# Linear attention block on one core: two sequences in turn, both chunks' scores and both chunks' weighted sums in one run each

## The chip, the core and the metric

The kernel runs on one NeuronCore of a Trainium2 chip (trn2), as one launch. The metric is the device time of that core in microseconds (us). Engines are named as in the profile: PE is TensorE (its weight loads are PEld), DVE is VectorE, ACT is ScalarE, POOL is GpSimd, SP is SyncE, which here issues the DMAs. All data are float32.

## The reference

The input x has 4 sequences of 2048 positions and 512 features. A layer norm comes first, then an attention with gates and no softmax, then a second layer norm and a feed-forward part of low rank, both with a residual. Cut to what matters (`gate` is divided by its mean over the features):

```python
xn = layernorm(layernorm(x)) * ln_g + ln_b           # outer and inner norm
q, k, v = split(xn @ W_qkv + b_qkv)
gate = sigmoid(layernorm(x) @ W_gate + b_gate)
q = relu(q * gate) ** 2 + EPS                        # 16 heads of 32
k = relu(k * gate) ** 2 + EPS
# along the sequence, for each head:
kv_s += k_t[:, None] * v_t[None, :];  k_s += k_t
out_t = (q_t @ kv_s) / (q_t @ k_s + EPS)
x = x + out @ W_proj + b_proj
x = x + gelu(layernorm(x) @ U1 @ V1 + b1) @ U2 @ V2 + b2
```

The recurrence couples positions within a sequence only; the four sequences are independent of each other.

## The kernel before

The 8192 rows are cut into 64 chunks of 128 positions, 16 to a sequence. The recurrence is computed by chunks. Within a chunk the scores (keys times queries, 16 small products of 32 rows by 128 columns, each two records on PE) are masked to the causal triangle on DVE (`scores_of`, L611) and multiplied with v; what came before the chunk enters as queries times the state S (`weighted`, L672); then S is brought up to date by k times v, accumulated in a PSUM bank of its own over a whole sequence and copied out after each chunk. The denominators come from a running sum of the keys (a scan on DVE, `sums_of`, L590) times the queries (POOL), summed over heads (`inverse_denominators`, L637).

The main loop (L1140) goes in steps of two chunks, c and c + 1, which before the change follow each other in one sequence. The large products of a pair of chunks are done by a scheme with seven half products in place of eight: `gates_and_values` and `queries_and_keys` (L435, L480; all at L426, seven groups each) and `project_two_out` (L762). A step does the following on PE, in this order: gates and values of c, c + 1; scores of e = c - 1; queries and keys of c, c + 1; `down` of the feed-forward part (ps_P, L844); rest of the attention of e (products with S, with v, state update); some feed-forward items; output projection of c - 2 and c - 1; scores of c; the other feed-forward items; rest of the attention of c; the two products `up` (ps_u, L883). So c + 1 has its scores and its rest a step later.

The feed-forward part works on blocks of two chunks (`feed_forward`, L837). It is a list of closures that `pump(n)` takes from, n at a time: `down`, then 16 products `hidden` (ps_h, L859), each followed by a gelu on ACT (L861), and 16 products `gather` (ps_Q, L865), each two behind its `hidden`; then two `up`, which also write the result out.

Queries, keys and normalized features are needed with features in partitions. They are turned over by a transpose of 32 by 32 blocks on DVE (L286), a write to DRAM (L302, L325) and reads back (L307: four reads of 32 partitions each; L330: one read of a chunk). `turned_in_quarters` issues the write and then every read that stands in the list `back` (`transfers_back`), and appends its own reads to that list. So a tile's reads are issued on SP behind the next write. `features_back` issues the reads of the next pair's features (xlT). The keys read back (kq) go through ACT (`keys_of`, L583: plus EPS, in order of time), then the scan and the scores.

The order of instructions on each engine is written out by hand (`manual_schedule`): each engine and SP's queue work in the order of the program, and semaphores make an instruction wait for what it reads and for buffers. PSUM before: 6 banks under one tag, one for the feed-forward sum (acc) and one for the state (S).

Of the kernel before, what the change touches and what calls it, by code (L numbers as in the profile page):

```python
# [60 lines left out]
def tile_linear_attention_block(  # L61
# [45 lines left out]
    def bank(name):  # L107
        return psum.tile([P, 512], F32, tag="bank", bufs=6, name=name)
# [3 lines left out]

    def load_x(c):
        t = xp.tile([P, D], F32, tag="x", name=f"x_{c}")
        nc.sync.dma_start(t, xf[bass.ts(c, P), :])
        x_of[c] = t
# [32 lines left out]
    bg_one = row(b_gate, "a", 4, "bg_one", nc.scalar)  # L149
# [25 lines left out]
    bqkv_one = [row(b_qkv[bass.ts(n, D)], "a", 4, f"bqkv_one_{n}", nc.sync) for n in range(3)]  # L175
# [236 lines left out]

    def combinations(c):
# [21 lines left out]
    def gates_and_values(c, s, meanwhile):  # L435
# [6 lines left out]
        nc.scalar.copy(t1, ps1)  # L442
        ps2 = bank(f"ps_gu_{c}")
        half_product(ps2, s[:, 1], wgv, T2)
        u2 = temp(f"gu2_{c}")
        nc.vector.tensor_add(u2, ps2, t1)
        ps5 = bank(f"ps_g_{c + 1}")
# [3 lines left out]
        meanwhile()  # L451
# [3 lines left out]
        done = [sigmoid_of(c, g0)]  # L455
        half_product(ps5, b[:, hi], wgv, T4, more=True)
# [11 lines left out]
        nc.vector.tensor_add(t5, ps3, bqkv_row[:, 2 * D : 3 * D])  # L468
        ps4 = bank(f"ps_v_{c}")
# [10 lines left out]
    def queries_and_keys(c, s, first=None, factors=None, queries=None, later=None):  # L480
# [9 lines left out]
        def square(c, n, t):  # L490
# [6 lines left out]
            sq = work.tile([P, D], F32, tag="k", bufs=3, name=f"k_{c}")  # L497
# [7 lines left out]
        if first:  # L505
            first()
# [5 lines left out]
        if factors:  # L512
            factors()
        nc.vector.tensor_add(t1, ps1, bq)
        q0 = square(c, 0, t1)
        if queries:
            queries()
# [5 lines left out]
        nc.gpsimd.tensor_add(u4, u2, t5)  # L523
        qT0 = turn_queries(c, q0)
# [4 lines left out]
        if later:  # L529
            later()  # L530
# [4 lines left out]
        nc.gpsimd.tensor_add(u3, u3, t5)  # L535
        half(ps5, b[:, NH:NK], T4, more=True)
        kq0 = turn_keys(c, k0)
        nc.vector.tensor_add(u2, ps5, u2)
        q1 = square(c + 1, 0, u2)
        k1 = square(c + 1, 1, u3)  # L540
        transfers_back()

        def second():
            qT1 = turn_queries(c + 1, q1)
            kq1 = turn_keys(c + 1, k1)
            pairs[c + 1] = k1, qT1, kq1
# [9 lines left out]
    def new_values(c):  # L556
        return work.tile([P, D], F32, tag="v", bufs=3, name=f"v_{c}")


    state = {"S": None, "sums": None, "bank": None}  # L560

    def turn_queries(c, q):
        qT = work.tile([P, NQ, NK, DH], F32, tag="qT", bufs=3, name=f"qT_{c}")
        turned_in_quarters(q, qT, f"q_{c}")
        return qT
# [7 lines left out]
    def new_keys(c):  # L573
        kT = work.tile([P, NK, P + 1], F32, tag="kT", bufs=2, name=f"kT_{c}")
        if c % SEQ == 0:
            nc.gpsimd.memset(kT[:, :, 0:1], 0.0)
        else:
            nc.gpsimd.tensor_copy(kT[:, :, 0:1], state["sums"][:, :, P : P + 1])  # L578
        return kT
# [10 lines left out]
    def sums_of(c, kT, qT):  # L590

        sums = work.tile([P, NK, P + 1], F32, tag="sums", name=f"sums_{c}")
        flat = "p g t -> p (g t)"
# [8 lines left out]
        state["sums"] = sums  # L602
        qs = work.tile([P, NK, P], F32, tag="qsum", name=f"qsum_{c}")
        nc.gpsimd.tensor_mul(  # L604
            qs.rearrange("p k (i t) -> p k i t", t=DH),
            qT.rearrange("p i k t -> p k i t"),
            sums[:, :, 1 : P + 1].rearrange("p k (i t) -> p k i t", t=DH),
# [3 lines left out]
    def scores_of(c, qT, kT):  # L611
# [3 lines left out]
        for g in range(NK):  # L615
            for r in range(HG):
# [7 lines left out]
                )  # L624
        scores = []
        for r in range(HG):
            a = work.tile([P, NK, P], F32, tag="a", bufs=4, name=f"a_{c}_{r}")
# [9 lines left out]
    def inverse_denominators(c, qs):  # L637

        back = work.tile([P, NK, P], F32, tag="back", name=f"back_{c}")
        nc.vector.transpose(back.rearrange("p g t -> p (g t)"), qs.rearrange("p g t -> p (g t)"))  # L640
        den = work.tile([P, H], F32, tag="den", bufs=2, name=f"den_{c}")
# [11 lines left out]
        den = inverse  # L653
        inv = work.tile([P, NK, P], F32, tag="back", name=f"inv_{c}")
        nc.vector.transpose(
            inv.rearrange("p g t -> p (g t)"), den.unsqueeze(2).to_broadcast([P, H, DH])
# [15 lines left out]
    def weighted(c, scores, qT, k, v, inv):  # L672


        S = state["S"]
        first = c % SEQ == 0

        num = [bank(f"ps_n_{c}"), bank(f"ps_m_{c}")]  # L680

        def place(g, r):
            at = r ^ (g % 2 * 2)
            return num[g % 2][at * DH : (at + 1) * DH, bass.ts(g // 2, P)]

        if not first:
            for g in range(NK):
                for r in range(HG):
                    rows = slice(r * DH, (r + 1) * DH)
                    nc.tensor.matmul(  # L690
                        place(g, r),
                        S[rows, g, :],
                        qT[rows, :, g, :],
                        start=(g < 2),
                        stop=False,
                        skip_group_check=True,
                    )
        for g in range(NK):
            for r in range(HG):
                h = g * HG + r  # L700
                nc.tensor.matmul(
                    place(g, r),
                    v[:, h * DH : (h + 1) * DH],
                    scores[r][:, g, :],
                    start=first and g < 2,
# [3 lines left out]
        if inv is None:  # L709
            return num  # L710
        oT = numerators_over(c, num, inv)


        if c % SEQ != SEQ - 1:
            if first:
                state["bank"] = psum.tile([P, 512], F32, tag="S", name=f"ps_S_{c}")
# [582 lines left out]
```

## Time and profile before

| what | value |
|---|---|
| time, median of 3 runs | 1780.97 us (1778.48 to 1781.12) |
| profiled execution, span from first to last instruction | 1778.1 us; no other time of it is given, so it is set beside the runs as 2.9 us under their median |
| PE busy | 1762.8 us, 99% |
| DVE, POOL, ACT busy | 1310.8, 832.4, 670.7 us |
| granted TensorE clock | 1.000 |
| DMA | 172.73 MB, mean 97 GB/s, 31.1% of 16 engines |
| a step of two chunks in steady state | 54.47 us |

The profile is one execution. Busy time counts an engine's instructions; the timelines list instructions of an engine in order of time, with start, length, source line, what is written from what, the shapes and how many records were merged. SP's lines are DMA issues, not transfers. The answer by windows gives, per stretch, its length, then the busy time and the instruction count of PE, PEld, DVE, ACT and POOL, then the granted clock, the DMA share of 16 engines and GB/s.

### The profile page before, as it was taken

What the parts mean: (1) busy time and instruction counts of PE and PEld (TensorE: products, weight loads), DVE (VectorE), ACT (ScalarE), POOL (GpSimd) and SP (SyncE); (2) the same over time, 40 slices, a digit from 0 to 9 for tenths busy, and PEclk for the clock granted to TensorE, in tenths of its full rate; (3) what the DMA queues carried; (4) which work ended last, traced back from release to release, by engine and by line L of the source; (5) the groups of instructions that cost most, each with busy time, mean ns of one, the idle gap of its engine ahead of it and who ended that gap; (6) DMA issues with size and microseconds to landing.
All of it is one profiled execution on the core that took longest, in us unless ns stands there. A gap on an engine that the chain in (4) does not pass through costs nothing.

```text
span 1778.1 us, 35487 instructions
## 1 busy us (share of the span) xinstructions
PE 1762.8 (99%) x13120; PEld 1135.1 (64%) x13120; DVE 1310.8 (74%) x2577; ACT 670.7 (38%) x1205; POOL 832.4 (47%) x1397
## 2 busy tenths in 40 slices
PE   9999999999999999999999999999999999999998
PEld 4555666656666666666566665666666666655677
DVE  7887777777777777777777777777777777777762
ACT  4333344333433333443334333333434343333333
POOL 3755455354553454543545534445435455344441
PEclk9999999999999999999999999999999999999999
DMA  7233332333323333323333233333233332332210
GB/s 231 80 101 92 104 101 91 98 95 100 108 87 97 103 91 105 101 91 98 92 103 103 91 98 104 90 107 101 88 99 93 104 102 90 97 103 79 85 61 24
DMA packets 284784, 172.73 MB, mean 97 GB/s; under 512 B 134590, under 2 KB 234430, under 8 KB 284484
## 3 DMA queue, kind: packets, MB, share of 16 engines
q1 hardware_dynamic: 283550, 170.46, 31.1%
q8 instruction: 104, 1.70, 0.4%
q14 instruction: 68, 0.56, 0.1%
q10 hardware_dynamic: 1062, 0.01, 0.0%
HBM read 89.15 MB, written 81.26 MB: 96 GB/s over the span
## 4 chain that ended last, share of the span: by engine, by line
PE 94%; DVE 3%; ACT 1%; DMA 1%; SPq 0%; issue 0%; POOL 0%; DVEq 0%; ACTq 0%; POOLq 0%
PE ps_h L859 13%; PE ps_Q L865 13%; PE ps_g L426 12%; PE ps_q L426 11%; PE ps_a L618 4%; PE ps_u L883 3%; PE ps_pt L426 3%; PE ps_pv L426 3%; PE ps_p L426 3%; PE ps_v L426 3%; PE ps_gt L426 3%; PE ps_u L426 3%; PE ps_gu L426 3%; PE ps_k L426 3%; PE ps_t L426 3%; PE ps_P L844 3%
## 5 line engine op out<-in xcount | busy, mean ns | idle before, releaser
L861 ACT ACTIVATE h<-ps_h,b_col 128x256 f32<-128x256 f32 x512 | 234.6, 470 | 331.1 <-PE ps_h L859 331.0
L859 PE MATMUL ps_h<-pT,v_sb 128*128 128x256 f32 x1024 | 300.5, 385 | 1.6 <-DVE pT L855 1.6
L865 PE MATMUL ps_Q<-h,u_sb 128*128 128x256 f32 x1024 | 298.6, 383 | 0.0
L604 POOL TENSOR_TENSOR qsum<-qT,sums 128x512 f32<-128x512 f32 x64 | 75.2, 1176 | 314.9 <-DVE sums L594 314.9
L865 PEld LDWEIGHTS ps_Q<-h,u_sb 128*128 128x128 f32 x1024 | 189.2, 190 | 40.4 <-ACT h L861 17.2
L859 PEld LDWEIGHTS ps_h<-pT,v_sb 128*128 128x128 f32 x1024 | 189.5, 190 | 32.1 <-DVE pT L855 3.0
L426 PE MATMUL ps_q<-wqk,xlT 128*128 128x512 f32 x372 | 177.9, 601 | 0.0
L628 DVE TENSOR_TENSOR a<-ps_a,causal 128x512 f32<-128x512 f32 x256 | 158.3, 680 | 23.5 <-PE ps_a L618 23.5
L426 PE MATMUL ps_g<-wgv,xlT 128*128 128x512 f32 x360 | 164.4, 592 | 0.0
L523 POOL TENSOR_TENSOR u<-u,t 128x512 f32<-128x512 f32 x32 | 40.6, 1268 | 208.6 <-DVE t L521 208.6
L570 POOL TENSOR_SCALAR k<-k 128x512 f32<-128x512 f32 x64 | 97.0, 1515 | 84.8 <-DVE blocks_k L286 84.8
L473 POOL TENSOR_TENSOR v<-gu,g 128x512 f32<-128x512 f32 x30 | 38.1, 1271 | 192.7 <-DVE g L468 192.7
L426 PEld LDWEIGHTS ps_g<-wgv,xlT 128*128 128x128 f32 x360 | 68.3, 190 | 85.7 <-issue 85.6
L426 PEld LDWEIGHTS ps_q<-wqk,xlT 128*128 128x128 f32 x372 | 68.1, 189 | 78.4 <-issue 53.1
L405 ACT ACTIVATE gate<-gate 128x512 f32<-128x512 f32 x64 | 40.3, 630 | 192.3 <-DVE gate L401 192.3
L494 ACT ACTIVATE t<-t,rg 128x512 f32<-128x512 f32 x32 | 23.1, 722 | 215.7 <-DVE t L492 215.7
L286 DVE STREAM_TRANSPOSE blocks_x<-x 128x512 f32<-128x512 f32 x60 | 42.0, 701 | 73.5 <-ACT x L267 73.5
L226 DVE BATCH_NORM_STATS2 st<-x 128x6 f32<-128x512 f32 x128 | 86.5, 676 | 8.6 <-DMA x<-in_L_attn_x_dram 6.4
L498 ACT ACTIVATE k<-u,rg 128x512 f32<-128x512 f32 x64 | 45.7, 714 | 120.7 <-DVE u L492 120.7
L594 DVE TENSOR_TENSOR_SCAN sums<-keep,kT 128x516 f32<-128x516 f32 x64 | 78.8, 1231 | 15.1 <-POOL kT L578 14.2
L618 PEld LDWEIGHTS ps_a<-qT,kT 32*128 32x128 f32 x2048 | 63.8, 186 | 35.9 <-issue 27.4
L982 POOL TENSOR_TENSOR x<-x,bp_row 128x512 f32<-128x512 f32 x64 | 81.4, 1272 | 0.0
(196 smaller groups left out, 3635.7 us busy)
## 6 DMA issues: line engine op xcount, KB each, us to landing
x<-in_L_attn_x_dram SPq DMA_DIRECT2D x64, 256.0 KB
dr_q<-blocks_q SPq DMA_DIRECT2D x64, 256.0 KB
dr_k<-blocks_k SPq DMA_DIRECT2D x64, 256.0 KB
qT<-dr_q SPq DMA_DIRECT2D x256, 64.0 KB
kq<-dr_k SPq DMA_DIRECT2D x256, 64.0 KB
out_dram<-x SPq DMA_DIRECT2D x64, 256.0 KB
dr_x<-blocks_x SPq DMA_DIRECT2D x60, 256.0 KB
x2T<-dr_x SPq DMA_DIRECT2D x240, 64.0 KB
```

The source lines that it names most:

```text
L226: nc.vector.bn_stats(st, src)
L426: nc.tensor.matmul(ps, stationary[:, k, :], w[:, slot, k, :], start=(k == 0 and not more), stop=(k == NH - 1), skip_group_check=True,)
L570: nc.gpsimd.tensor_scalar_add(k, k, EPS)
L594: nc.vector.tensor_tensor_scan(sums.rearrange(flat), keep.rearrange(flat), kT.rearrange(flat), 0.0, ALU.mult, ALU.add,)
L604: nc.gpsimd.tensor_mul(qs.rearrange("p k (i t) -> p k i t", t=DH), qT.rearrange("p i k t -> p k i t"), sums[:, :, 1 : P + 1].rearrange("p ...
L618: nc.tensor.matmul(ps[r][:, bass.ts(g, P)], kT[rows, g, 1 : P + 1], qT[rows, :, g, :], start=True, stop=True,)
L628: nc.vector.tensor_tensor(a, ps[r].rearrange("p (g t) -> p g t", t=P), causal.unsqueeze(1).to_broadcast([P, NK, P]), ALU.mult,)
L844: nc.tensor.matmul(ps, u1_sb[:, k, :], x2T[:, :, :, k, :].rearrange("p j i t -> p (j i) t"), start=(k == 0), stop=(k == NK - 1),)
L859: nc.tensor.matmul(ps, v1_sb[:, 0, bass.ts(f, P)], held["p"], start=True, stop=True)
L861: nc.scalar.activation(h, ps, AF.Gelu_apprx_tanh, bias=b1_col[:, f : f + 1])
L865: nc.tensor.matmul(held["q"], u2_sb[:, f, :], held["h"].pop(f), start=(f == 0), stop=(f == NF - 1))
L982: nc.gpsimd.tensor_add(x_of[e], x_of[e], bp_row)
```

## The change

Chunks are numbered anew: two sequences run in turn, so that c and c + 1 are at the same time in two sequences (`rows_of_chunk`, used by the loads and stores of x). The state S and the carried sums of keys exist twice. In each step, now d = c - 2:

- the scores of c and c + 1 stand together near the end of the step, masked by eight operations on DVE into eight tiles (`a`, before four);
- the rest of the attention of d and d + 1 stands together in the gates of the next step: products with S for both, then for each chunk four products with v and four state updates in turn; the update goes to a bank taken for this step and is added to S in SBUF on DVE, in place of accumulating in PSUM;
- the output projection has another order, with three `hidden` behind its first half product; `down` stands within the queries and keys;
- the normalized features of the feed-forward part are turned in the gates, those of the next pair within the queries and keys;
- in `second`, keys go ahead of queries; keys and sums of c + 1 move into the step that made them;
- PSUM has 8 banks under one tag; ACT copies ps_Q.

```diff
+    def time_of(c):
+        return c % RUN // NS
+    def rows_of_chunk(c):
+        return bass.ts((c // RUN * NS + c % NS) * SEQ + time_of(c), P)
...
         def second():
+            kq1 = turn_keys(c + 1, k1)
             qT1 = turn_queries(c + 1, q1)
-            kq1 = turn_keys(c + 1, k1)
             pairs[c + 1] = k1, qT1, kq1
...
+        if time_of(c) != SEQ - 1:
+            carries[c] = work.tile([P, NK, 1], F32, tag="carry", bufs=2, name=f"carry_{c}")
+            nc.gpsimd.tensor_copy(carries[c], sums[:, :, P : P + 1])
+        qs = sums[:, :, 1 : P + 1]
...
+        for s in range(NS):
             for g in range(NK):
                 for r in range(HG):
+                    h = g * HG + r
                     nc.tensor.matmul(
+                        place(s, g, r),
+                        v[s][:, h * DH : (h + 1) * DH],
+                        scores[s][r][:, g, :],
...
+                if not last:
+                    add_to_state(s, g)
+            inv = spread_inverse(c + s, inverse[s])
+            out.append(numerators_over(c + s, num[s], inv))
+        if not last:
...
+                nc.vector.tensor_add(S, product, S)
...
+    def scores_in_step(c):
+        ps = [scores_of(n, pairs[n][1], keys.pop(n)) for n in (c, c + 1)]
+        scores[c] = [masked(c + n, p) for n, p in enumerate(ps)]
...
     for c in range(NJ, NC, 2):
-        e = c - 1
+        d = c - 2
+        def features_and_attention():
+            second_features()
+            rest_of_attention(d)
...
+            hooks = {4: features_and_attention}
+        gates_and_values(c, combos[c], hooks)
...
         rest += feed_forward((c - 4) // NP)
+        second = queries_and_keys(
+            c,
+            combos.pop(c),
+            {
+                1: lambda: run(normalize_pair(c + 2)),
+                5: lambda: pump(1),
+                6: lambda: combine_results(d),
+            },
+        )
+        features_back()
         second()
+        for n in (c, c + 1):
+            keys[n] = new_keys(n)
+        project_two_in_step(d, lambda: pump(3))
+        transfers_back()
         for n in (c + 4, c + 5):
             first_moments(n)
...
         if c + 2 < NC:
             combine(c + 2)
+        pump(5)
+        sums_and_products(c)
+        pump(4)
+        denominators_in_step(c)
+        pump(10)
+        sums_and_products(c + 1)
+        waiting += second_norm([d, d + 1], mv_second, others, mv_first)
+        for n in (c, c + 1):
+            offset_in_residual(n)
+        pump(len(rest) - NP)
+        scores_in_step(c)
+        denominators_in_step(c + 1)
+        if c + 2 == NC:
+            second_features()
+        pump(len(rest))
```

A hook's number tells after which half product of the seven it runs. `sums_and_products(n)` issues `keys_of` on ACT, the scan on DVE and the product with the queries on POOL.

## The prediction

> **What bounds the kernel now.** I read the page's busy times first, then TensorE's timeline over one step, then SyncE's (SP's) timeline over the same step, then the DMA share by microsecond.
>
> ```profile
> PE 1762.8 (99%) x13120; PEld 1135.1 (64%) x13120; DVE 1310.8 (74%) x2577; ACT 670.7 (38%) x1205; POOL 832.4 (47%) x1397
> ```
>
> PE has 15 us of idle time in 1778.1. So two things can move the time: work leaves PE, or a wait appears in front of it. The table of waits puts no wait of PE in the steady steps over 0.4 us.
>
> TensorE's timeline (start, length, line, what, records) around the second chunk's attention and one run of scores:
>
> ```profile
> 770.96 1.89 PE L844 MATMUL ps_P<-x2T,u_sb 128*128 128x256 f32 x8
> ...
> 773.13 0.29 PE L690 MATMUL ps_n<-qT,S 32*32 32x128 f32 x4
> ...
> 773.38 0.42 PE L701 MATMUL ps_n<-a,v 128*32 128x128 f32 x8
> 773.62 0.40 PE L701 MATMUL ps_m<-a,v 128*32 128x128 f32 x8
> ...
> 774.27 0.49 PE L720 MATMUL ps_S<-v,k 128*32 128x32 f32 x32
> 774.73 1.56 PE L859 MATMUL ps_h<-pT,v_sb 128*128 128x256 f32 x6
> ...
> 786.74 0.59 PE L865 MATMUL ps_Q<-h,u_sb 128*128 128x256 f32 x2
> 787.26 1.17 PE L618 MATMUL ps_a<-qT,kT 32*128 32x128 f32 x32
> 788.36 0.70 PE L859 MATMUL ps_h<-pT,v_sb 128*128 128x256 f32 x2
> 788.90 0.59 PE L865 MATMUL ps_Q<-h,u_sb 128*128 128x256 f32 x2
> ```
>
> To be seen: two L865 records take 0.43 us, so the scores were due at 787.17 and start at 787.26; after them the first full-array product takes 0.54 (788.36 to 788.90) in place of 0.43. Every change of the array's tiling costs time at its edges.
>
> SP's timeline, same step. I call T0 the end of the products of queries and keys, 770.96:
>
> ```profile
> 772.46 0.33 SPq L302 DMA_DIRECT2D dr_k<-blocks_k  x1
> 772.95 2.25 SPq L307 DMA_DIRECT2D qT<-dr_q  x4
> 775.32 2.17 SPq L307 DMA_DIRECT2D kq<-dr_k  x4
> 777.61 2.32 SPq L330 DMA_DIRECT2D xlT<-drn_xl  x2
> 780.03 0.67 SPq L302 DMA_DIRECT2D dr_q<-blocks_q  x1
> 780.79 0.38 SPq L302 DMA_DIRECT2D dr_k<-blocks_k  x1
> 787.96 2.19 SPq L307 DMA_DIRECT2D qT<-dr_q  x4
> 790.26 2.26 SPq L307 DMA_DIRECT2D kq<-dr_k  x4
> ```
>
> To be seen: the write of the second chunk's queries, issued at 780.03, has landed only at 787.96, when SP may issue the reads. SP's table of waits has this each step ("DMA dr_q<-blocks_q: 212.4, 33, 8.0"). The DMA share by microsecond, where 0.25 is 4 of 16 engines:
>
> ```profile
> 785.00:786.00 1.00, 1.00 (x6) 0.89 (x5) 0.86 (x2) 0.73 (x2) 0.00 (x0) 1.00 0.27 84
> ...
> 792.00:793.00 1.00, 1.00 (x6) 0.87 (x5) 0.90 (x5) 0.61 (x2) 0.72 (x4) 1.00 0.25 76
> ...
> 795.00:796.00 1.00, 1.00 (x6) 0.79 (x5) 0.00 (x0) 0.80 (x2) 1.00 (x2) 1.00 0.22 65
> 796.00:797.00 1.00, 1.00 (x38) 0.47 (x40) 0.59 (x1) 1.00 (x3) 0.92 (x2) 1.00 0.02 6
> ```
>
> The eight quarter-reads run from 789 to 796 at a share of 0.25: about 3.5 us for four, and whatever waits behind them on those engines waits its turn. In the last step, which reads no xlT, the same reads are issued at 1708.12, 11.7 us after its ps_P at 1696.4; here it is 17.0. So the two xlT reads delay what follows them by 5.3 us. Today nobody needs these chunks before the next step.
>
> **The change, part by part.**
>
> *Scores of both chunks together.* A run costs, from when it is due (787.17) to when the second product after it has its usual place (788.90 - 0.43 = 788.47), 1.30 us. Its steady part I take from the products with v, which also stream 128 columns on four tiles: 8 records in 0.22 (773.62, 773.84 and on), so 32 in 0.88. Two runs in one save 1.30 - 0.88 = 0.42 us per step, on PE.
>
> *The rest of both together.* One run now lasts from 772.69 (770.96 + 8 x 0.216) to 774.73, plus 0.11 for the slow first product: 2.15. Steady parts: products with S 8 records in 0.11, so 0.44; with v 0.88; state updates 0.30 from first start to last (0.49 less 0.196, one record's length). Sum 1.62; the second run in the same block saves 0.53 us.
>
> *State updates among products with v.* Same number of records, and both are 128*32 tiles; the border from L701 to L720 shows no gap (774.06 + 0.22 = 774.28, start 774.27). The border back, L720 to L701, hardly stands in the trace. Bounds: a gain of 0.3 per chunk if the updates hide wholly, a loss of 0.11 per border (one load of L720) x 4 x 2 = 0.9 per step. I take 0, by the border that is shown. The Trainium skill (TensorE: Matmul & The Clock Gate, section on packing small matmuls) says that a weight load overlaps running matmuls only where the row group differs; these tiles use all four row groups, so by it every load would show, 0.11 x 32 = 3.5 us per chunk for the products with v alone. The trace has 0.88 for them, so the row decides.
>
> *PE's other work is the same* in kind and number. The wait of 0.25 after the first three ps_h (774.73 to 776.27 for 1.30 of work) loses most of its cause, as output products now follow them: 0.15. Gain on PE together 0.42 + 0.53 + 0.15 = 1.1 us; a step of 54.47 (ps_u starts at 689.41 and 743.88) would be 53.4 without new waits.
>
> *DVE* loses a copy (two of 0.28 become one add, 0.42 by the row of half-bank adds); *POOL* gains a carry copy per chunk (0.19), *ACT* the copy of ps_Q (0.37). All beside PE: cover is DVE's idle quarter and ACT's 62%. Without cover they'd cost about 1 us per step.
>
> *The feature transfers of x2T* move to the fourth hook of the gates; ps_P follows 17 us later on PE. The normalization waits for the gate's sigmoid, 2 us into that; write and eight reads take some 11 (2 x 0.7 transposes, 2 to land, 7 of reads). Slack about 4 us: nothing.
>
> *Keys and scores of c+1 move into their own step.* This is the new wait. Before, L583 for c+1 stood at the step's end (796.99) and its scores in the next step (812.21). After, PE has from T0: one half product 0.86, three ps_h 1.30, six half products 5.19, then 5 + 4 + 10 feed-forward items of 0.432 = 8.2: at T0 + 15.6 the keys of c+1 are queued on ACT. ACT works in order: the gelu of ps_h 12 and all later ones stand behind. PE has five more items (h12, g10, h13, g11, h14: 2.16) and at T0 + 17.7 it needs that gelu.
> When do the keys come? SP's order is kept: dr_k (T0 + 1.5), reads of qT and kq, two xlT reads, then the second chunk's writes at T0 + 9.1. The keys now go first, so their reads take the place of those at 787.96: T0 + 17.0. Four reads last till about 792.6 (half of 789 to 796): T0 + 21.7. Then L583 0.71, gelu 0.47, some 0.3 for hand-overs: T0 + 23.2. PE stands still 5.5 us. Behind it wait the last gathers, both scores and ps_u; the scan on DVE also waits, with nothing but masks behind it. The second qT lands by the same rows at T0 + 25.2 (796.1); the scores of c+1, then due at about T0 + 26.5, just escape. Even with keys on time, that qT alone would hold them from T0 + 20.9 to 25.2, 4.3 us: two waits with one cause.
> Bounds of the stall: 4.0 (reads a microsecond earlier, no hand-overs) to 6.5 (write landing at 8.0, the longest wait).
> As to the rule: the Trainium skill (DMA: Bandwidth & Descriptors, Bandwidth) gives 2.0 us plus bytes at 436 GB/s for a DMA, 2.6 for 256 KB. By it the keys' write would land at about T0 + 12 and the keys at T0 + 15, before ACT asks, and the change would be worth its 1.1 us per step, some 1748 in all. The row at 787.96 stands against it.
>
> *Clock.* The granted clock is 1.00 all through. At the start, the first eight ps_g took 5.98 us where eight later ones took 3.70 (chain of waits, 9.37 and 16.46): a cold array costs 2.28. An idle gap of 2.61 us (before ps_P at 118.12) cost nothing: its eight records took 1.97. A gap of 5.5 lies beyond what is shown; bounds 0 and 2.28 per step, I take half, 1.15. The Trainium skill (TensorE: Matmul & The Clock Gate, Part 1) puts the idle window at about 3.4 us; by it such a gap slows PE in many steps, not in all.
>
> **Sum.** A step is 53.4 + 5.5 = 58.9 (+4.4), with the clock +5.55. Steps c = 4 to 60 read xlT: 29. 29 x 5.55 = 161; the last step gains 1.1; prologue and tail have the same work in another order, 0 with bounds of 10 either way. 1778.1 + 160 = 1938; the runs' median lies 2.9 above the span: 1941, rounded to 1940. Without clock loss 1907, with all of it 1974.
>
> **The rivals.**
> *No wait (faster):* the second chunk's keys land before T0 + 16.5 and its queries before T0 + 20.9. Then 30 x 1.1 = 33 us are won: 1748. For it speaks the last step's 11.7 us; against it, that this step alone has no xlT reads ahead, while SP's order in the others stays. It decides at about 5 us less. Chance 0.08.
> *A shorter wait* of 1.2 to 4 us, if the landing of the first write runs ahead of the second xlT read: 1785 to 1860. 0.10; a wait of 1.1, which cancels the gain, 0.02.
> *More than one wait:* a slow clock in every step and exposed loads at the borders (0.9): 29 x (4.4 + 2.28 + 0.9) = 220, so 2000 and up. 0.08.
> *Forecast:* 0.72, its own range 1865 to 1985.
>
> The range takes the forecast and the upper part of the shorter wait: 1860 to 1990. Faster 0.08, same 0.02, slower 0.90, where 0.2% (3.6 us) is about what a measurement of this kernel can tell from no change.
>
> **What would show it.** Right: PE idle some 5 us before L865-type records in each step, released by ACT's gelu, with ACT idle before the keys' activation, released by a DMA of kq; PE busy near 92%; score runs of 64 records in 2.2 us or less. Wrong: PE at 98 to 99% and steps of 53.4 (no wait), or gaps inside the v and update records, or before ps_P (x2T late), or a wait that sits at the scores alone.

## Result and the profile after

The changed kernel takes 2014.59 us, median of four runs (2010.96 to 2023.08), against 1779.72 (1778.39 to 1781.12) for the kernel before on the same chip: ratio 1.1329, 95% interval 1.1302 to 1.1357. Slower was forecast, 1940 us and at most 1990. The profiled execution spans 2009.1 us, against 1778.1.

The page's busy times, then, in the table of waits (us in total, times, longest), PE's two largest and ACT's for the keys:

```profile
PE 1813.1 (90%) x13120; PEld 1173.4 (58%) x13120; DVE 1319.6 (66%) x2515; ACT 673.6 (34%) x1237; POOL 880.8 (44%) x1457
```

```profile
PE ps_Q L891 <- ACT h L887: 158.0, 44, 6.1
PE ps_S L723 <- issue: 7.5, 7, 1.8
```

```profile
ACT kT L597 <- DMA kq<-dr_k: 219.3, 63, 7.0
```

PE executes as many records as before and is idle for 196 us in place of 15. It is also busy for 50 us more. So there are two losses: a wait, in which `gather` (L891, L865 before) stands for a gelu, and PE working at a slower pace. The mean granted clock is 0.950, where it was 1.000. A third, small line is new: 7.5 us in front of the state updates, which the profile ascribes to no releaser ("issue").

One step shows the wait; T0, the end of the products of queries and keys, is at 815.2. SP's timeline:

```profile
816.92 0.33 SPq L311 DMA_DIRECT2D dr_k<-blocks_k  x1
...
822.34 1.58 SPq L339 DMA_DIRECT2D xlT<-drn_xl  x2
824.02 0.61 SPq L311 DMA_DIRECT2D dr_k<-blocks_k  x1
824.73 0.38 SPq L311 DMA_DIRECT2D dr_q<-blocks_q  x1
832.00 2.19 SPq L316 DMA_DIRECT2D kq<-dr_k  x4
834.30 2.29 SPq L316 DMA_DIRECT2D qT<-dr_q  x4
```

The second chunk's keys are written behind the two reads of xlT, and the write has landed only 8.0 us later, when the reads start at T0 + 16.8. ACT's timeline, then PE's:

```profile
837.70 0.72 ACT L597 ACTIVATE kT<-kq,eps_col 128x512 f32<-128x512 f32 x1 [6.02 <-DMA kq<-dr_k]
838.33 1.19 ACT L887 ACTIVATE h<-ps_h,b_col 128x256 f32<-128x256 f32 x3
```

```profile
832.67 0.59 PE L891 MATMUL ps_Q<-h,u_sb 128*128 128x256 f32 x2
833.11 0.59 PE L885 MATMUL ps_h<-pT,v_sb 128*128 128x256 f32 x2
838.83 1.22 PE L891 MATMUL ps_Q<-h,u_sb 128*128 128x256 f32 x2 [5.13 <-ACT h L887]
839.85 1.06 PE L885 MATMUL ps_h<-pT,v_sb 128*128 128x256 f32 x2
840.70 2.53 PE L891 MATMUL ps_Q<-h,u_sb 128*128 128x256 f32 x6
843.16 2.07 PE L635 MATMUL ps_a<-qT,kT 32*128 32x128 f32 x64
```

The keys' activation is at T0 + 22.5, three gelus queue behind it, and PE stands still for 5.13 us. Then ten full-array records take 4.33 us, from 838.83 to 843.16, where ten at full speed take 2.16 (about 0.43 for two, as between the starts at 832.67 and 833.11). The answer by windows gives the reason in the seventh group after the window, the clock (then DMA share and GB/s):

```profile
833.00:834.00 1.00, 0.70 (x4) 0.27 (x2) 0.00 (x0) 0.00 (x0) 1.00 (x2) 1.00 0.17 52
838.00:839.00 1.00, 0.17 (x1) 0.17 (x2) 0.59 (x2) 1.00 (x3) 0.00 (x0) 0.50 0.29 86
841.00:842.00 1.00, 1.00 (x4) 0.73 (x4) 0.00 (x0) 0.47 (x1) 0.95 (x1) 0.50 0.02 8
845.00:846.00 1.00, 1.00 (x11) 0.52 (x7) 1.00 (x3) 0.00 (x0) 0.71 (x4) 1.00 0.00 0
```

PE comes out of the gap at half its clock. It does so in every one of the 29 steps that read xlT: the records of the clock give half speed once in each, for 3.4 or 6.8 us (here from 836.0, still within the gap, to 842.8), 188 us in these steps.

What the change was said to save on PE is saved. Both chunks' scores take 2.1 us, as the line at 843.16 shows, and the rest of both chunks is one block. PE's timeline in the step before, its first and last parts:

```profile
793.78 0.43 PE L737 MATMUL ps_n<-a,v 128*32 128x128 f32 x8
794.02 0.24 PE L723 MATMUL ps_S<-v,k 128*32 128x32 f32 x8
794.08 0.41 PE L737 MATMUL ps_m<-a,v 128*32 128x128 f32 x8
...
795.99 0.24 PE L723 MATMUL ps_S<-v,k 128*32 128x32 f32 x8
796.16 1.12 PE L438 MATMUL ps_g<-wgv,xlT 128*128 128x512 f32 x2
```

Eight groups of products and updates take 2.38 us, 793.78 to 796.16; by the prediction's rows it was 2 x (0.88 + 0.30) = 2.36 with borders at nothing.

**The account.** Counted from one first record of ps_P to the next, a step has a mean length of 61.85 us over the 29 that read xlT, against 54.42 before (54.47 is the usual one, some are shorter): 29 x 7.43 = 215 us. Outside those steps the span is 1778.1 - 29 x 54.42 = 199.9 before and 2009.1 - 29 x 61.85 = 215.5 after: 16 us, of which 8.0 lie ahead of the first ps_P (118.1 before, 126.1 after). Together 231, the difference of the spans.

### The profile page after: what moved, and what is told of

Its sections match the earlier page's. It is cut to its first block, busy times and chain, and to the rows that moved or that the text cites. A ratio compares the mean times of both kernels' runs of the same rounds, so it can differ in the third digit from the quotient of the medians.

```text
span 2009.1 us, 35689 instructions
## 1 busy us (share of the span) xinstructions
PE 1813.1 (90%) x13120; PEld 1173.4 (58%) x13120; DVE 1319.6 (66%) x2515; ACT 673.6 (34%) x1237; POOL 880.8 (44%) x1457
## 4 chain that ended last, share of the span: by engine, by line
PE 69%; DMA 17%; DVE 5%; issue 3%; SPq 2%; POOL 1%; ACT 1%; ACTq 0%; DVEq 0%; POOLq 0%
DMA dr_k<-blocks_k 12%; PE ps_q L438 10%; PE ps_g L438 10%; PE ps_Q L891 6%; DMA kq<-dr_k 5%; PE ps_h L885 4%; PE ps_a L635 3%; PE ps_u L906 3%; PE ps_p L438 3%; PE ps_P L870 3%; PE ps_t L438 3%; PE ps_k L438 3%; PE ps_u L438 3%; PE ps_gu L438 2%; PE ps_v L438 2%
## 5 line engine op out<-in xcount | busy, mean ns | idle before, releaser
L891 PE MATMUL ps_Q<-h,u_sb 128*128 128x256 f32 x1024 | 347.9, 438 | 158.7 <-ACT h L887 158.0
L891 PEld LDWEIGHTS ps_Q<-h,u_sb 128*128 128x128 f32 x1024 | 219.1, 220 | 216.4 <-ACT h L887 182.5
L887 ACT ACTIVATE h<-ps_h,b_col 128x256 f32<-128x256 f32 x512 | 222.3, 471 | 216.6 <-PE ps_h L885 216.4
L885 PEld LDWEIGHTS ps_h<-pT,v_sb 128*128 128x128 f32 x1024 | 202.8, 198 | 32.1 <-DVE pT L881 1.9
L660 DVE STREAM_TRANSPOSE back<-sums 128x512 f32<-128x512 f32 x64 | 45.1, 705 | 222.4 <-POOL sums L621 222.4
L430 POOL TENSOR_TENSOR combos<-xlT 128x256 f32<-128x256 f32 x31 | 22.5, 726 | 320.5 <-DMA xlT<-drn_xl 242.0
L850 POOL TENSOR_TENSOR x<-x,b_row 128x512 f32<-128x512 f32 x64 | 80.4, 1279 | 185.4 <-ACT x L276 185.4
L597 ACT ACTIVATE kT<-kq,eps_col 128x512 f32<-128x512 f32 x64 | 46.2, 722 | 219.3 <-DMA kq<-dr_k 219.3
L584 POOL TENSOR_SCALAR k<-k 128x512 f32<-128x512 f32 x64 | 107.9, 1699 | 6.1 <-DVE blocks_k L295 3.6
L621 POOL TENSOR_TENSOR sums<-qT,sums 128x512 f32<-128x512 f32 x64 | 74.9, 1171 | 45.8 <-DMA qT<-dr_q 35.5
```

What stands on the lines that cost most here:

```text
L584: nc.gpsimd.tensor_scalar_add(k, k, EPS)
L621: nc.gpsimd.tensor_mul(qs.rearrange(by_quarter, t=DH), qT.rearrange("p i k t -> p k i t"), qs.rearrange(by_quarter, t=DH),)
L850: nc.gpsimd.tensor_add(xt, xt, b2_row)
L885: nc.tensor.matmul(ps, v1_sb[:, 0, bass.ts(f, P)], held["p"], start=True, stop=True)
L887: nc.scalar.activation(h, ps, AF.Gelu_apprx_tanh, bias=b1_col[:, f : f + 1])
L891: nc.tensor.matmul(held["q"], u2_sb[:, f, :], held["h"].pop(f), start=(f == 0), stop=(f == NF - 1))
```

## Experiments

The first four runs ask what makes PE stand and what it costs, a fifth (queries first) turns one part of the change back, and the others try the version without the wait and its parts. Ratios are to the kernel before on the same chip, whose median was between 1779.3 and 1780.5 us each time.

**Features last.** The reads of xlT go behind the second chunk's transfers, and the sums for the gates, which read xlT, are formed later.

```diff
-        features_back()
         second()
...
         transfers_back()
+        features_back()
...
-        if c + 2 < NC:
-            combine(c + 2)
...
         sums_and_products(c + 1)
+        if c + 2 < NC:
+            combine(c + 2)
```

> The reads of the next pair's features (xlT) are issued behind the reads of the second chunk's keys and queries, and the sums on POOL that need them stand behind the keys' sums. Theory A (the new wait comes from the keys of c + 1, which queue behind the two xlT reads on a quarter of the DMA engines): their write lands at about T0 + 11, the first read is issued there, L597 for c + 1 starts at about T0 + 16 instead of 22.5, the gap before ps_Q falls from 5.2 us to under 0.7, the granted clock stays at 1.00; a step is 53.5 to 54.3 us, the run 1765 to 1795 us. Theory B (the gap comes from ACT's order or from PSUM banks of the merged scores, whatever the DMAs do): gap and time as they are, 2000 to 2020 us.

Measured: 1840.69 us, ratio 1.0347 (1.0327 to 1.0368), clock 0.996, a step 55.93. SP's timeline in a step with T0 at 747.7, and the new wait of PE's weight loads:

```profile
755.19 0.60 SPq L311 DMA_DIRECT2D dr_k<-blocks_k  x1
755.89 0.38 SPq L311 DMA_DIRECT2D dr_q<-blocks_q  x1
759.52 2.19 SPq L316 DMA_DIRECT2D kq<-dr_k  x4
```

```profile
PEld ps_gu L438 <- POOL combos L431: 46.4, 29, 2.2
```

The second chunk's keys are read from T0 + 11.8 and not from T0 + 17; the gap ahead of `gather` falls from 5.2 us to 0.2 in the mean, and no step is at half clock any more. Moving the two reads in SP's queue, with the sums that need them, brings 174 of the 235 us. The run misses its expected time by 46 us, above all by a wait that the move makes: xlT now lands about T0 + 25, and the gates of the next step stand for the sums formed from it, 0.77 us of PE per step. With 0.56 that is left ahead of `gather`, most of it at the first chunk's keys, and 0.36 in gaps without a releaser, that is 1.7 of the 2.5 us by which the step exceeds the 53.43 reached below; the rest is in no gap above 50 ns and stays open.

**Features spread.** xlT is still read first, but each chunk as four reads of 32 partitions. The source then has 32 rows as its slowest dimension, where it had 4.

```diff
+            for j in range(NQ):
                 nc.sync.dma_start(
-                    new_tile().rearrange("p k t -> p (k t)"),
-                    dr.rearrange("m j k i t -> j m (k i t)"),
+                    to[j * DH : (j + 1) * DH, :],
+                    dr[:, j].rearrange("m k i t -> m (k i t)"),
                 )
```

> The place of the xlT reads is kept, but each is issued as four reads of 32 partitions, whose slowest dimension is 32 and no longer 4. Theory A1 (a read whose slowest dimension is 4 runs on 4 engines, and the second chunk's writes wait behind it on those): DMA share in the xlT reads well over 0.5, SP spends about 2 us more on issues, the second chunk's write still lands 3 to 4 us earlier, gap about 1.6 us, clock near 1.00, 1810 to 1850 us. Theory A2 (the xlT reads delay by their bytes or by the order of the queue, on however many engines): the landing stays at T0 + 17 or later, 2000 to 2060 us.

Measured: 1894.6 us, ratio 1.0647 (1.0629 to 1.0664). First the share of the 16 DMA engines (windows, last figures but one) while the xlT reads are under way, in the changed kernel and in this run, then SP's timeline in this run (T0 at 769.2):

```profile
828.00:830.00 2.00, 2.00 (x11) 1.77 (x10) 0.52 (x1) 1.02 (x3) 0.00 (x0) 1.00 0.26 99
```

```profile
777.20:779.20 2.00, 2.00 (x11) 1.77 (x10) 1.83 (x5) 0.95 (x2) 0.00 (x0) 1.00 0.69 178
```

```profile
776.33 4.15 SPq L341 DMA_DIRECT2D xlT<-drn_xl  x8
780.58 0.37 SPq L311 DMA_DIRECT2D dr_k<-blocks_k  x1
781.04 0.38 SPq L311 DMA_DIRECT2D dr_q<-blocks_q  x1
782.72 2.19 SPq L316 DMA_DIRECT2D kq<-dr_k  x4
```

The write behind the reads lands after 2.1 us in place of 8.0. Part of that is a later issue: eight issues of 0.52 us keep SP until 780.5, so the write is issued 2.6 us later in the step than in the changed kernel (T0 + 11.4 against 8.8). Counted from the first issue of the xlT reads, the keys' reads start after 6.4 us in place of 9.7, with the same bytes ahead of them: what held the write was the reads' tail on some 4 of 16 engines, not their bytes.

A gap of about 2 us stays, where 1.6 was expected, and the clock is not near 1.00 throughout: 14 of the 29 steps have half clock, 13 of them after gaps of 1.92 to 2.61 us. The run misses its range by these two. Two gaps of the same length in PE's timeline, and a window behind each (the clock is the third figure from the end):

```profile
848.28 0.70 PE L894 MATMUL ps_Q<-h,u_sb 128*128 128x256 f32 x2 [2.61 <-ACT h L890]
```

```profile
1601.22 0.70 PE L894 MATMUL ps_Q<-h,u_sb 128*128 128x256 f32 x2 [2.61 <-ACT h L890]
```

```profile
849.00:851.00 2.00, 2.00 (x17) 1.40 (x20) 0.14 (x1) 0.70 (x2) 0.83 (x2) 1.00 0.08 24
1602.00:1604.00 2.00, 2.00 (x6) 1.65 (x5) 0.07 (x1) 0.47 (x1) 0.93 (x2) 0.50 0.09 26
```

Of the 22 steps whose longest gap lies between 1.92 and 2.64 us, 13 have half clock and nine do not; of the six with 1.40 to 1.85 us none has.

The Trainium skill (DMA: Bandwidth & Descriptors, "Why a DMA increments its semaphore by 16 and not by 1") says that a copy runs on the largest number of engines, up to 16, that divides the slowest dimensions of both sides; 4 and 32 rows would then give 4 and 16 engines, which the share of 0.26 there and 0.69 here, more than 4 of 16 could give, agree with. The reads of keys and queries also have 4 in that place in the code (each takes 32 rows of the DRAM tile and writes all 128 partitions), and ran at 0.25 in the prediction's windows; no run spread those.

**Keys after the feed-forward items.** The keys and sums of c + 1 go back on ACT, to just ahead of the scores.

```diff
         pump(10)
-        sums_and_products(c + 1)
...
         pump(len(rest) - NP)
+        sums_and_products(c + 1)
         scores_in_step(c)
```

> The keys and sums of c + 1 are queued on ACT, DVE and POOL only behind the last gelu, just ahead of the scores; DMAs as in the change. Theory A (two waits with one cause): the gelus run through, the gap before ps_Q goes, and PE stands at the scores instead, because kq is on time for them only at about T0 + 23 and the second qT lands at T0 + 25.5: a gap of 3 to 5 us there; step 60 to 62 us, 1970 to 2020 us. Theory B (the place on ACT's queue is the fault): without the keys ahead of the gelus the time falls to 1760 to 1850 us.

Measured: 1995.13 us, ratio 1.1207 (1.1190 to 1.1224). PE's timeline, T0 at 804.9:

```profile
825.18 1.17 PE L635 MATMUL ps_a<-qT,kT 32*128 32x128 f32 x32
831.04 2.09 PE L635 MATMUL ps_a<-qT,kT 32*128 32x128 f32 x32 [4.69 <-DMA qT<-dr_q]
```

The wait behind the second chunk's keys is gone from `gather` (0.27 us per step is left, at the first chunk's), and the second chunk's scores stand for its queries instead: 4.69 us here, 130.2 in all by the table of waits, against 158.0. Half clock follows in each of the 29 steps, after gaps of 3.55 to 5.36 us. Reordering ACT moves the wait and hardly shortens it; that both waits have one cause is shown by the run with the features last, where both go.

**Gap filled.** Eleven products that nobody reads (two records each, 638 in all) go where PE would stand still.

```diff
         for n in (c, c + 1):
             offset_in_residual(n)
+        pump(5)
+        if c + 2 < NC:
+            spare = bank(f"ps_spare_{c}")[:, 0:BT]
+            for _ in range(11):
+                nc.tensor.matmul(
+                    spare, u1_sb[:, 0, :], v2_sb[:, 0, 0:BT], start=True, stop=True
+                )
         pump(len(rest) - NP)
```

> Eleven products of 128x256 (4.75 us by their rows) that nobody reads stand on PE in front of the gather that waits, in each step but the last. Theory A with the clock as a second loss: PE is busy in the gap, the granted clock stays at 1.00, the gap falls to about 0.5 us, and a step loses the 1.9 us that the slow clock costs: about 60 us, 1945 to 1975 us, though PE does 140 us more work. Theory C (the slow clock costs little, and the excess over the forecast lies elsewhere): 2000 us or more, up to 2150 if PE is what bounds.

Measured: 1960.21 us, ratio 1.1012 (1.0996 to 1.1029), clock 0.995. The page:

```profile
PE 1891.6 (97%) x13758; PEld 1250.7 (64%) x13758; DVE 1326.8 (68%) x2515; ACT 673.7 (34%) x1237; POOL 880.4 (45%) x1457
```

PE does 638 x 0.216 = 138 us more work, and the kernel is 54 us faster than the changed one, 1.9 us per step. Work and the gaps that are left take 4.75 + 0.72 us of a step, about what the gap took (5.22), so what is won is what a gap costs beyond its own length; with PE kept busy no step is at half clock. From the traces: between the gap's end and ps_u stand ten full-array records and the scores, 6.50 us on average in the changed kernel; in the run with both moves below, six records and the scores take 3.49, so ten would take 4.35. That makes a loss of 2.15 us per step to the clock.

**Queries first.** One part of the change undone: the second chunk's queries are turned ahead of its keys, as in the kernel before.

```diff
         def second():
-            kq1 = turn_keys(c + 1, k1)
             qT1 = turn_queries(c + 1, q1)
+            kq1 = turn_keys(c + 1, k1)
```

> The changed kernel with one part undone: the second chunk's queries are turned before its keys, as in the kernel before. Theory A (SP's queue decides: whichever write stands first behind the xlT reads is read from T0 + 17, the other's four reads 2.4 us later): the second chunk's keys land about 2.4 to 4 us later, the gap of PE grows from 5.2 to some 8 us, a step is 2.4 to 4 us longer, 2085 to 2130 us. Theory B (the keys land when the DMA engines are free, whatever the order of issue): no change, 2005 to 2025 us.

Measured: 2114.78 us, ratio 1.1877 (1.1859 to 1.1894), a step 65.20. SP's timeline, T0 at 845.6:

```profile
854.01 1.08 SPq L311 DMA_DIRECT2D dr_q<-blocks_q  x1
855.19 0.38 SPq L311 DMA_DIRECT2D dr_k<-blocks_k  x1
862.69 2.19 SPq L316 DMA_DIRECT2D qT<-dr_q  x4
864.99 2.72 SPq L316 DMA_DIRECT2D kq<-dr_k  x4
```

Now the queries are read from T0 + 17.1 and the keys from T0 + 19.4; the gap is 8.35 us in this step. So the part "keys ahead of queries" works as written and is worth 100 us here, about 3.4 per step: it shortens a wait that the rest of the change makes.

**Both moves.** Features last and spread, and the keys of c four feed-forward items later (`pump(9)` in place of `pump(5)` ahead of them, `pump(8)` in place of `pump(10)` behind).

> The reads of xlT stand behind the reads of the second chunk's keys and queries, as in the run with the features last, and each goes as four reads of 32 partitions; the combinations for the gates stand behind the sums of c+1, and the keys of c stand four feed-forward items later. Theory A (every wait of the changed kernel comes from the place of these reads in SP's queue and from keys asked for too early): in the run with the features last 1.4 us of a step were left in front of the gates and up to 1.4 in front of the first chunk's keys. xlT landed there about 25 us after T0; with 16 engines in place of 4 it lands about 4 us earlier, and both waits go. A step is then 53.4 to 54.2 us; with a prologue and tail 16 us longer than before, and 9 us of gaps that no wait explains, 1765 to 1795 us: within 1% of the kernel before. Theory B (the waits in front of the gates come from DVE and POOL being late, not from a DMA): the step stays at 55 to 56, 1825 to 1845 us.

Measured: 1789.11 us, ratio 1.0048 (1.0035 to 1.0061), a mean step of 54.10, and 53.43 in the steps without a gap, which is the step of 53.4 that the prediction gave for the change without new waits. So 225 of the 235 us hung on transfers and on when they were asked for. What remains: outside the steps 1787.6 - 29 x 54.10 = 218.7 us in place of 199.9, and within them nine gaps in the block of small products, 9.8 us, for which no releaser is shown. One of them in PE's timeline:

```profile
220.22 0.41 PE L740 MATMUL ps_m<-a,v 128*32 128x128 f32 x8
222.11 0.27 PE L726 MATMUL ps_S<-v,k 128*32 128x32 f32 x8 [1.49 <-issue]
```

All nine end 2.2 to 2.9 us after a packet of 16 KB began on the queue that the page calls "instruction" (q8, 104 such packets). Ten of the 29 blocks of small products are under way 2.2 to 2.9 us after such a packet began, and nine of these have the gap; of the other 19 none has. The kernel before, whose blocks are half as long, has no such gap, though 15 of its 58 blocks are under way at such a time. The next run asks about that.

**Rest in two parts.** As with both moves, but the fifth half product of the gates (four records, 1.7 us of the whole array) stands between one chunk's products with v and updates and the other's.

> As the run with both moves, but a half product of the gates stands between the weighted sums of one chunk and those of the other, so that the block of small products is in two parts. Theory A (the gaps in the block that no wait explains come from instructions of PE that are still being fetched, as small products use them up faster than they come): most of the about 9 us of these gaps go, and two more edges cost 0.5 us per step, 15 us: 0 to 10 us slower than the run with both moves, with under 3 us of such gaps. Theory B (the gaps have another cause, such as the banks of PSUM): they stay at 8 to 10 us, and the run is 13 to 18 us slower.

Measured: 1786.43 us, ratio 1.0033 (1.0022 to 1.0044). No gap without a releaser is left in the block in any of the 29 steps. Two more edges cost 53.76 - 53.43 = 0.33 us per step and not 0.5. That the gaps go when full-size products cut the block in two, and that each had followed such a packet, fits instructions that are used up faster than they are fetched; no run changed the fetching itself.

**Updates apart.** As with both moves, with each chunk's state updates behind all its products with v.

> As the run with both moves, but the state updates of a chunk stand behind its four groups of products with v and not among them. Theory A (a border between the two kinds of 128x32 tiles costs nothing, as the prediction took it): within 0.2 us per step, 6 us in all, of the run with both moves. Theory B (the updates hide among the products with v): up to 0.6 us per step slower, 18 us. Theory C (every border exposes a weight load of 0.11 us): six borders fewer per step, 0.6 to 0.7 us, 20 us faster.

Measured: 1790.63 us, ratio 1.0060 (1.0047 to 1.0072), not told apart from the run with both moves; a step without a gap is 53.56 in place of 53.43. The borders between the two kinds of tile cost nothing that shows, and the interleaving as such brings about 0.1 us per step.

**Scores apart.** As with both moves, with the scores and masks of c fourteen feed-forward items ahead of those of c + 1 (six ahead of the keys and sums of c + 1, which is the six that the expectation counts).

> As the run with both moves, but the scores and masks of c stand six feed-forward items earlier than those of c+1: two runs of scores per step in place of one. Theory A (a run of scores costs 0.42 us at its edges, as the prediction took it from the profile before): 30 x 0.42 = 13 us slower than the run with both moves. Theory B (the masks of eight tiles in a row hold back what DVE does next, and come apart better): equal or up to 10 us faster.

Measured: 1805.91 us, ratio 1.0144 (1.0131 to 1.0157): 16.8 us slower, 0.58 for each of 29 steps, of which 0.22 is a gap ahead of a `hidden` that this order also brings. A step without other gaps is 54.33 in place of 53.43, 0.90 with the same gap in it. So a run of scores costs between 0.36 and 0.68, around the 0.42 that the prediction gave it.

**Edges.** Rest in two parts, with one change in the step (sums of c + 1 one item later), two in the prologue (the first scores of chunk 1 later; feature transposes ahead of denominators) and one in the tail (five items behind the last projection and not ahead of it).

> As the run with the rest in two parts, with four places at the edges and one in the step changed: in the prologue the scores of chunk 1 stand two half products later than those of chunk 0, so that the reads of its queries have time (a gap of 4.2 us, and an array at half clock behind it, 1.6 us); ahead of the rest of chunks 2 and 3 the feature transposes stand before the denominators, which wait 1.5 us for POOL; in the tail five feed-forward items that stood before the last output projection stand behind it (a gap of 4.9 us, five items are 2.2 us); the sums of c+1 stand one item later (gaps of 0.2 to 1.1 us in some steps, 3 us in all). Theory A (these gaps are waits of PE alone): 7 to 12 us faster than the run with the rest in two parts, 1775 to 1780 us. Theory B (the prologue is bound by DVE, which works without a pause there): only the tail and the steps gain, 3 to 5 us, 1781 to 1784 us.

Measured: 1784.9 us, ratio 1.0029 (1.0020 to 1.0039). A gain of 1.5 us where 3 to 12 were expected, and within the uncertainty of both runs. PE's waits:

```profile
PE ps_q L441 <- DVE t L530: 6.9, 2, 6.3
PE ps_x L285 <- ACT x L276: 5.4, 1, 5.4
```

In the prologue the wait for the second chunk's queries fell from 4.2 to 1.2 us, and the later wait for DVE rose from 5.1 to 6.3: that fits the theory of a bound DVE. The tail's edit was in the wrong place: its wait, up from 4.9 to 5.4, stands in the last step of the loop, ahead of the feature transposes (L285), before any of the five items that were moved.

**Tail.** Rest in two parts, with the sums of c + 1 one item later, and in the last step the feature transposes ahead of the last scores.

```diff
-        scores_in_step(c)
-        denominators_in_step(c + 1)
         if c + 2 == NC:
             second_features()
+        scores_in_step(c)
+        denominators_in_step(c + 1)
```

> As the run with the rest in two parts (not the run with the edges), with the sums of c+1 one item later, as there, and one place in the tail: in the last step of the loop the feature transposes stand ahead of the last scores and not behind them. Theory A (the 4.9 us that PE stands in the last step, and 1.7 us at half clock behind it, come from transposes that queue behind eight masks of 4.9 us): 6 us less, and 1 to 2 us from the steps: 1777 to 1781 us, no difference from the kernel before that can be told. Theory B (the wait moves to the rest of the last chunks, which needs the masks): 0 to 2 us, 1784 to 1787 us.

Measured: 1789.01 us, ratio 1.0054 (1.0041 to 1.0068), 2.6 us slower than rest in two parts, little beyond the uncertainty of the two. PE's waits, then ACT's timeline in the last step:

```profile
PE ps_x L285 <- ACT x L276: 7.2, 1, 7.2
...
PE ps_h L897 <- DVE pT L893: 4.2, 2, 3.7
```

```profile
1720.59 1.52 ACT L276 ACTIVATE x<-x,shift_f,rs_f 128x512 f32<-128x512 f32 x2 [5.96 <-POOL shift_f L270]
```

The transposes do not queue behind the masks: they wait for a normalization on ACT, and that for its factors from POOL. Asked for earlier, they wait longer, 7.2 us, and what DVE does behind the scores, first the masks, is later now and holds PE a second time, 3.7 us. Theory B was right in kind (the wait moves to what stands behind the masks), and the price higher than it said. No version that was run beats the kernel before: in this one the steps win 29 x (54.42 - 53.90) = 15 us, and the ends lose 1787.2 - 29 x 53.90 - 199.9 = 24.

## Why the prediction was wrong in size

**What held.** The mechanism and its place: PE idle ahead of `gather`, released by a gelu behind the keys' activation, which waits for a DMA that stands behind two xlT reads in SP's queue. The chain in numbers, forecast and then measured mean, as T0 plus us: reads of the second chunk's keys 17.0, 17.2; keys' activation 21.7, 22.6; `gather` resumes 23.2, 23.8; gap 5.5, 5.22. The step without new waits 53.4, 53.43; that it agrees so closely is in part luck, as one of its parts, the rest of both chunks in one block, measured 0.33 us (rest in two parts) where 0.53 had been put, and the scores 0.36 to 0.68. That the second wait, for the queries, lay just behind the first was borne out by the run with keys after the feed-forward items. The rule which the prediction weighed, 2.0 us plus bytes at 436 GB/s, gave 1748; the write took 8.0 us, so the row was the better guide. The page gives this rule in its section "Anatomy of one DMA — SWDGE (gpsimd) path", as a fit for DMAs issued from GpSimd; those here are issued on SP, and the write stood behind other reads.

**What failed: two terms of the sum and two that it did not have, all in one direction.**

- *The clock.* Taken at half of its bound, 1.15 us per step; it was 2.15, nearly all of the 2.28 that the first products had lost at the start (the first record of the clock begins at 14.0 us, when most of these products had run). The prediction knew a gap of 2.61 us that cost nothing and had no row near 5.5; it took the half, where the upper bound was the better estimate. 29 x 1.0 = 29 us. The free gap proved less than it seemed: in the run with the features spread such gaps were free in nine of 22 steps. The Trainium skill (TensorE: Matmul & The Clock Gate, Part 1) gives 1.2 GHz after at least one idle window of about 3.4 us in a free-running count. The half clock here lasts one or two times 3.4 us, which agrees; the prediction's inference from it, that many steps but not all would be slow, does not: with a gap of 5.2 us all were. Nor was an idle gap of a whole such window needed here: half clock also came after 13 gaps of 1.92 to 2.61 us, and the measurement decides.
- *Prologue and tail.* Taken at nothing, with bounds of 10 for both; they cost 16 us. The prologue's first scores wait 4.2 us for a DMA, as the second chunk's scores now stand in the step that makes its queries; 5.1 us are lost later behind DVE; in the last step feature transposes wait 4.0 us, put down to the masks there and to ACT's normalization in the later runs. The run with both moves and those built on it keep 16 to 24 us here.
- *Gaps in the block of small products.* In no term of the sum (they were named only as a sign of being wrong), 0.30 us per step, 9 us.
- *Earlier keys.* The first chunk's keys also go through ACT in a place where PE soon needs a gelu: 0.23 us per step, 7 us. The prediction looked only at the second chunk's.

The step then comes to 53.43 + 5.22 + 2.15 + 0.30 + 0.23 = 61.33; 0.5 us of the measured 61.85 is in no gap above 50 ns and stays unplaced. The forecast's step was 60.05. The difference of 1.8, 29 times, is 52 us; with 16 at the ends that is 68 of the 71 us between the forecast span of 1938 and the measured 2009.1. Most of the rest is the 1.1 us that the last step was to gain and the 54.47 that stood for a mean of 54.42. The range failed on its own terms, too: the bounds that the prediction gave for the gap, the clock and the ends reach 1781 + 29 x (6.5 + 2.28 - 1.1) - 1 + 10 = 2013 us together (1781 is 1778.1 + 2.9), and the range stopped at 1990. The median of the runs lay 5.5 us above the span and not 2.9.

**The rivals.** No wait and a shorter wait are refuted by the gaps of 4.6 to 6.1 us. "More than one wait" named 2000 us and up, and is where the time fell, in part by luck: of its parts the clock was right, exposed loads at the borders were not there, and the ends and the smaller gaps made up for them. The forecast gave 0.72 to the middle of a term whose ends were 0 and 2.28. The records show the clock in full or in half and nothing between, so the middle is what comes of half of the steps being slow; that is the case of gaps near 2 us, not of 5.

## What to carry to other kernels

Work taken from the bounding engine counts only as long as nothing new is asked for earlier: follow each moved consumer back to the DMA it reads, then to what stands ahead of that in the issuing queue, and put long reads that nobody needs soon behind the short transfers that somebody does. One free gap in a trace does not show that gaps of its length are free: here 1.9 to 2.6 us brought half clock in 13 of 22 steps, and 3.55 us or more in every step. A gap on PE clearly longer than the free ones should be priced at its length plus the whole of the cold-clock cost seen elsewhere in the trace, not at half of it. Where a loop's steps are rearranged, the prologue and tail are sums of their own: 16 us here, half of the 33 that the change could win.

## What the runs showed of the hardware

- After an idle gap of 3.55 us or more PE's granted clock was 0.50 in every step (the changed kernel, 4.6 to 6.1 us; keys after the feed-forward items, 3.55 to 5.36; queries first, 7.9 to 9.4); after 1.92 to 2.64 us in 13 of 22 steps (features spread); after 1.85 us or less in none of that run, and 2.61 us in the kernel before cost nothing.
- A write behind two reads with 4 rows in the slowest dimension landed after 8.0 us (DMA share 0.26), behind reads of the same bytes with 32 rows after 2.1 us (share 0.69); from the first issue of the reads to the landing it was 9.7 and 6.4 us.
- In the merged block of small products on PE (run with both moves) there are 0.4 to 1.6 us without a releaser in nine of 29 steps, each ending 2.2 to 2.9 us after a 16 KB instruction packet began; with full-array products in the middle of the block, none.
